# Layer 0's cross-attention: one ring of eight PSUM banks, and maxima and exponentials of two heads at a time

## The chip, the cores and the metric

The kernel runs on one core of a Trainium2 chip. Five engines share the work: TensorE (PE; PEld is its loading of weights), VectorE (DVE), ScalarE (ACT), GpSimd (POOL) and SyncE (SP). The metric is device time in microseconds. The kernel before took 2884.81 us, the median of three runs (2878.84 to 2887.44).

## The reference

A decoder of two layers on 32 sequences of 100 tokens of width 256, all in float32. Each layer is self-attention, cross-attention to a context of 361 rows of width 128, and a feed-forward part with experts, each on a layer norm and with a residual. The change lies in the cross-attention of layer 0, with 16 heads of 16:

```
Q = (x @ Wq.T).reshape(B, xN, NUM_HEADS, HEAD_DIM)
KV = (z @ Wkv.T).reshape(B, zN, 2, NUM_HEADS, HEAD_DIM)
K = KV[:, :, 0]
V = KV[:, :, 1]
attn = jnp.einsum('bqhd,bkhd->bhqk', Q, K) * SCALE
attn = jax.nn.softmax(attn, axis=-1)
O = jnp.einsum('bhqk,bkhd->bqhd', attn, V).reshape(B, xN, DIM)
return O @ Wo.T
```

## The kernel before, in words

The method `l0_xattn` does this part. T is 100 tokens, L is 361 context rows, which are also held as NKC = 3 chunks of KC0 = 121, and P is 128 partitions. Weights (`wB`), context (`cT`, three buffers, loaded two sequences ahead on SP's queue), keys `ks`, values `vs` and the negated maxima `ms` (three buffers each) lie in SBUF.

The 16 heads of a sequence are worked on in four groups: `c` chooses eight heads, and `j` the even or the odd ones of them. The four heads of one `j` lie in four groups of 32 partitions, so that four matmuls with 32 rows can run beside each other. A loop over `M` = 2b + c has 64 full turns for 32 sequences `b`, and two more that finish. The softmax takes the scores twice: once as tokens by context rows, to get each token's maximum, and once turned, as context rows by tokens, with the maximum already subtracted through the query. One turn of the loop issues on PE, in this order:

- `maxima(M - 1)` (L585): two transposes of the negated maxima, which DVE adds to the query (L587, tile `q2`).
- `scores(M, 0)`: four matmuls into four PSUM banks (128 partitions by 512 float32 each), `k,qT` in the profile. DVE reduces each bank to its negated maximum (L577).
- `turned(M - 1, 0)`: twelve matmuls into four banks, `q,k` in the profile; they need `q2`. ACT takes the exponential of each bank (L599, tile `e`), POOL adds two and then the third chunk (L603, L604, tile `es`).
- `values(M - 2)`: the products with the values (L613) and the sums of exponentials (L620) into one bank, which ACT copies (L625, tile `zs`). DVE takes a reciprocal (L630) and POOL multiplies (L634) in a later turn.
- `scores(M, 1)` and `turned(M - 1, 1)`: the same for the other half, j = 1.
- Extras: `keys` of the next sequence (`cT,wB` in the profile; ACT copies them, L549) always first; for c = 0 the output projection of an earlier tile (`wB,zT`; DVE adds it, L283) and two chunks of `vals` (`wB,cT`; ACT copies them, L562); for c = 1 `queries` in half of the sequences (L542) and the third chunk of `vals`. In some turns a tile's norm is turned (L253) or its gates are computed (L1517 and on).

The order on PE is that of the program, written out by hand (`manual_schedule`); the order on DVE, ACT and POOL is set by a scheduler, which keeps the dependencies. The eight PSUM banks are one pool with the tag `t`: `bank()` hands out the next of eight buffers, whatever it is for, and a buffer's next user waits until all users of the one before are done with it. L178 is the line of the helper `mm`, which issues most matmuls, so the operands' names tell them apart.

Of the kernel before, what the change touches and what calls it, by code (L numbers as in the profile page):

```python
# [9 lines left out]
F32 = mybir.dt.float32  # L10
I32 = mybir.dt.int32
U32 = mybir.dt.uint32
AF = mybir.ActivationFunctionType
ALU = mybir.AluOpType
AX = mybir.AxisListType

P = 128
NB = 32
T = 100
# [5 lines left out]
L = 361  # L25
NKC = 3
KC0, KC = 121, 124
# [94 lines left out]
class Kernel:  # L122
    def __init__(self, ctx, tc, a):
        self.ctx, self.tc, self.nc, self.a = ctx, tc, tc.nc, a
        nc = tc.nc
        self.n_evac = self.stored = 0
        self.const = ctx.enter_context(tc.tile_pool(name="const", bufs=1))
        self.wts = ctx.enter_context(tc.tile_pool(name="wts", bufs=1))
        self.lnp = ctx.enter_context(tc.tile_pool(name="ln", bufs=2))
        self.norms, self.norm_of, self.norm_after = {}, {}, None  # L130
        self.x = self.const.tile([P, NF, D], F32, tag="x", name="x_sb")
        xd = a["x"].rearrange("b t d -> (b t) d").rearrange("(f p) d -> p f d", p=P)

        def load_x(f, n=4):
            n = min(n, NF - f)
            nc.sync.dma_start(self.x[:, f : f + n, :], xd[:, f : f + n, :])

        self.load_x = load_x
        load_x(0, 2)
        load_x(2, 2)  # L140
        self.xnT = self.const.tile([P, NK, NT], F32, tag="xnT", name="xnT")
        self.ident = self.const.tile([P, P], F32, tag="ident", name="ident")
        make_identity(nc, self.ident)


    def banks(self, name, **n):

        self.n_banks = n
        return self.tc.tile_pool(name=f"ps{name}", bufs=1, space=bass.MemoryType.PSUM)

    def bank(self, tag):
        if tag not in self.n_banks:
            tag = "t"
        return self.psum.tile([P, 512], F32, tag=tag, name=f"ps_{tag}", bufs=self.n_banks[tag])
# [315 lines left out]
    def l0_xattn(self):  # L470
        nc, tc, a = self.nc, self.tc, self.a
        with ExitStack() as st:
            self.psum = st.enter_context(self.banks("l0x", t=8))
            w = self.wts.tile([P, 3584], F32, tag="wB", name="wB0")
            wq = w[:, :512].rearrange("p (k n) -> p k n", k=NK)
            wk, wv = w[:, 512:768], w[:, 768:1024]
# [40 lines left out]
            ks = [cp.tile([P, 2, 2, LP0], F32, tag=f"k{i}", name=f"k{i}") for i in range(3)]  # L517
            ms = [cp.tile([T, 2, P], F32, tag=f"m{i}", name=f"m{i}") for i in range(3)]
# [9 lines left out]
            ctx, q, q2, e, es = {}, {}, {}, {}, {}  # L528
            self.z_begin(pool, 2)

            def load(b):
                ctx[b] = pool.tile([CD, LP], F32, tag="cT", name="cT", bufs=3)
                nc.sync.dma_start(ctx[b], a["ctxT"][:, b, :])

            def queries(b0, c):
                if c == 0:
                    q[b0 // 4] = pool.tile([P, 2, 2, 4 * T], F32, tag="qT", name="qT")
                pm = self.bank_t()[:, : 4 * T]
                self.mm(pm, [(wq[:, k, c * P : (c + 1) * P], self.xn_of(k, b0, 4)) for k in range(NK)])
                t = q[b0 // 4]  # L540
                for j in range(2):
                    nc.scalar.activation(t[:, c, j, :], pm, AF.Copy, scale=quarter[:, j : j + 1])  # L542

            def keys(b, c):
                pm = self.bank_t()[:, :L]
                self.mm(pm, [(wk[:, c * P : (c + 1) * P], ctx[b][:, :L])])
                t = ks[b % 3]
                for j in range(2):
                    nc.scalar.activation(  # L549
                        t[:, c, j, :L], pm, AF.Identity, bias=one[:, j : j + 1], scale=own[:, j : j + 1]  # L550
                    )

            def vals(b, c0, n):
                pm = self.bank_t()[:KC0, : n * D].rearrange("p (c d) -> p c d", c=n)
                for i in range(n):
                    c = c0 + i
                    self.mm(pm[:, i, :], [(ctx[b][:, c * KC0 : (c + 1) * KC0], wv)])
                pv = pm.rearrange("p c (h j d) -> p c h j d", j=2, d=16)
                v = vs[b % 3][:, c0 : c0 + n].rearrange("p c (h j) e -> p c h j e", j=2)
                for j in range(2):  # L560
                    for i in range(n):
                        nc.scalar.copy(v[:, i, :, j, 16 * j : 16 * j + 16], pv[:, i, :, j, :])  # L562

            def rows_of(r):
                return slice(32 * r, 32 * r + 32)


            def scores(M, j):
                b, c = divmod(M, 2)
                cols = slice((b % 4) * T, (b % 4 + 1) * T)  # L570
                ps = [self.bank("r")[:T, :L] for _ in range(4)]
                for r in range(4):
                    self.mm(ps[r], [(q[b // 4][rows_of(r), c, j, cols], ks[b % 3][rows_of(r), c, j, :L])])
                m = ms[M % 3]
                for r in range(4):
                    o = 32 * r + 16 * (1 - j)
                    got = nc.vector.tensor_reduce(m[:, j, o : o + 1], ps[r], AX.X, ALU.max, negate=True)  # L577
                return got

            def maxima(M):  # L580
# [7 lines left out]

            def turned(M, j):
                b, c = divmod(M, 2)  # L590
                ps = [self.bank("r")[:KC0, : NKC * T] for _ in range(4)]
                for i in range(NKC):
                    for r in range(4):
                        self.mm(ps[r][:, i * T : (i + 1) * T], [(
                            ks[b % 3][rows_of(r), c, j, i * KC0 : (i + 1) * KC0], q2[M][rows_of(r), j, :]
                        )])
                t = e[M, j] = pool.tile([KC0, 4, NKC, T], F32, tag="e", name="e", bufs=5)
                for r in range(4):
                    nc.scalar.activation(t[:, r], ps[r].rearrange("p (c t) -> p c t", c=NKC), AF.Exp)  # L599

                n = L - 2 * KC0
                s = es[M, j] = pool.tile([KC0, 4, T], F32, tag="es", name="es", bufs=4)
                nc.gpsimd.tensor_tensor(s, t[:, :, 0, :], t[:, :, 1, :], ALU.add)  # L603
                nc.gpsimd.tensor_tensor(s[:n], s[:n], t[:n, :, 2, :], ALU.add)  # L604
# [31 lines left out]
            def out(f):  # L636
                self.out_proj(f, wo)
                self.norm_stats(f, EDGES)
# [37 lines left out]
            with tc.manual_schedule(engines={mybir.EngineType.PE}):  # L676
                load(0)
                load(1)
                for c in range(2):
                    queries(0, c)  # L680
                for c in range(2):
                    keys(0, c)
                vals(0, 0, 2)
                vals(0, 2, 1)
                last = 2 * NB
                for M in range(last + 2):
                    b, c = divmod(M, 2)
                    if c == 0:
                        if b + 2 < NB:
                            load(b + 2)  # L690
                        ex = extras(b)
                    if 0 < M <= last:
                        maxima(M - 1)
                    if M in norms:
                        f, *at = norms[M]
                        f(*at)
                    for j in range(2):

                        got = scores(M, j) if M < last else None
                        if j == 0 and M > 2:  # L700
                            divided(M - 3, zs, got)
                        if 0 < M <= last:
                            turned(M - 1, j)
                        if j == 0 and M > 1:
                            zs = values(M - 2)
                    if M == last + 1:
                        divided(M - 2, zs, None)
                    for i in (0, 2, 1):
                        if ex[3 * c + i]:
                            ex[3 * c + i]()  # L710
                    if M not in norms or len(later) > 3:
                        for _ in range(1 + (len(later) > 3)):
                            if later:
                                later.popleft()()
                out(NF - 1)
                while later:
                    later.popleft()()


    def l1_xattn_weights(self):  # L720
# [1484 lines left out]
```

## Time and profile before

| | |
|---|---|
| median of three runs | 2884.81 us (2878.84 to 2887.44) |
| the profiled execution | 2912.63 us, its span 2910.9 us |
| busy over the span | PE 96%, DVE 60%, ACT 48%, POOL 32% |
| granted clock, mean | 0.982 |
| the loop of this part | about 536 to 1011 us of the span |
| maxima, L577 | 512 instructions, 525 ns each, 239.6 us busy |
| exponentials, L599 | 512 instructions, 425 ns each, 173.8 us busy |
| copies of values, L562 | 192 instructions, 300 ns each, 40.0 us busy |

Times of single instructions are durations from start to end. Instructions that follow each other on DVE or ACT overlap, so that the distance of two starts is shorter than the duration. "Waits" name an engine that sat idle, the instruction that ended its idle time, the total in us, the number of times and the longest. Matmul ends are modelled, and so PE counts as busy a little longer than it is.

### The profile page before, as it was taken

The numbers are of one execution on the slowest core, as the hardware profiler recorded it, in microseconds if no ns is written. First come the engines' busy times: TensorE is split into PE (matmuls) and PEld (weight loads), VectorE is DVE, ScalarE is ACT, GpSimd is POOL, SyncE is SP. The second block draws the span as 40 slices with busy tenths as digits, with TensorE's granted clock in tenths as the row PEclk, the third lists the DMA queues.
The fourth block names the chain that finished last, engine by engine and source line by source line (L and its number), as shares of the span: only waits on it lengthen the run. The fifth ranks groups of instructions, "written<-read, shape, count | busy, mean of one in ns | idle before, by whom it ended". The sixth has DMA issues, their size and how long they took to land. (4 is left out here: it accounts for less than half of the span.)

```text
span 2910.9 us, 66193 instructions
## 1 busy us (share of the span) xinstructions
PE 2793.5 (96%) x25908; PEld 2156.8 (74%) x25908; DVE 1760.9 (60%) x5057; ACT 1393.0 (48%) x4210; POOL 920.7 (32%) x1080
## 2 busy tenths in 40 slices
PE   8999999999999998999999999999999999999893
PEld 7888888777777756888885677777777777776672
DVE  7666666677777732222226877667676666776453
ACT  5465545666666611222223225656565556567120
POOL 3222212466565544222221230021311302223373
PEclk9999999999999999999999999999999999999997
DMA  7444333000000033655552000010000000000496
GB/s 246 128 142 151 131 139 120 21 16 16 16 15 14 5 120 117 205 196 199 209 206 86 24 2 10 9 45 19 23 15 9 15 9 14 10 12 6 116 215 188
DMA packets 130035, 235.44 MB, mean 81 GB/s; under 512 B 40074, under 2 KB 105285, under 8 KB 122928
## 3 DMA queue, kind: packets, MB, share of 16 engines
q1 hardware_dynamic: 99648, 136.98, 15.1%
q0 software_dynamic: 26784, 90.83, 9.7%
q8 instruction: 209, 3.42, 0.5%
q10 hardware_dynamic: 3280, 3.28, 0.3%
q14 instruction: 114, 0.93, 0.1%
HBM read 152.12 MB, written 111.18 MB: 90 GB/s over the span
## 5 line engine op out<-in xcount | busy, mean ns | idle before, releaser
L1801 POOL DMA_INDIRECT x_d<-xr,slot x200 | 195.0, 975 | 673.0 <-ACT eT L838 597.1
L178 PE MATMUL ps_t<-xnT,wA 128*128 128x200 f32 (+1 forms) x1608 | 322.5, 347 | 1.6 <-DMA wA<-in_wq 0.9
L178 PE MATMUL ps_t<-cT,q 128*128 128x361 f32 (+1 forms) x832 | 307.2, 472 | 0.0
L838 ACT COPY eT<-ps_t 124x384 f32<-124x384 f32 x400 | 191.5, 487 | 225.9 <-PE ps_t L837 220.7
L178 PEld LDWEIGHTS ps_t<-xnT,wA 128*128 128x128 f32 x1608 | 272.9, 191 | 29.5 <-issue 12.7
L828 ACT ACTIVATE wBx<-ps_t,m 128x361 f32<-128x361 f32 x400 | 227.8, 570 | 119.4 <-DVE m L825 109.9
L577 DVE TENSOR_REDUCE m<-ps_t 100x1 f32<-100x361 f32 x512 | 239.6, 525 | 48.5 <-PE ps_t L178 48.3
L178 PE MATMUL ps_t<-xT,w 128*128 128x256 f32 (+1 forms) x1276 | 260.2, 363 | 0.7 <-ACT xT L172 0.7
L178 PEld LDWEIGHTS ps_t<-xT,w 128*128 128x128 f32 x1276 | 223.6, 190 | 36.2 <-issue 9.3
L825 DVE TENSOR_REDUCE m<-ps_t 128x1 f32<-128x361 f32 x400 | 210.8, 528 | 59.9 <-PE ps_t L178 55.5
L837 PEld LDWEIGHTS ps_t<-ident,wBx 128*124 128x124 f32 x1200 | 150.3, 139 | 117.7 <-issue 71.0
L599 ACT ACTIVATE e<-ps_t 121x300 f32<-121x300 f32 x512 | 173.8, 425 | 120.7 <-PE ps_t L178 120.6
L384 ACT ACTIVATE e<-s,m 100x100 f32<-100x100 f32 x512 | 185.6, 364 | 66.2 <-DVE m L378 66.1
L388 POOL TENSOR_TENSOR e<-e,rz 100x400 f32<-100x400 f32 x128 | 109.1, 853 | 329.9 <-PE ps_t L178 218.7
L837 PE MATMUL ps_t<-ident,wBx 128*124 128x128 f32 x1200 | 196.7, 275 | 3.6 <-DVE top L1741 2.3
L178 PE MATMUL ps_t<-wA,cT 128*124 128x512 f32 x384 | 195.6, 597 | 0.0
L1448 DVE TENSOR_TENSOR h<-ps_t,g 128x256 f32<-128x256 f32 (+1 forms) x145 | 58.3, 402 | 188.4 <-ACT g L1447 180.0
L830 DVE TENSOR_SCALAR wBx<-wBx,sums 128x361 f32<-128x361 f32 x400 | 165.3, 413 | 9.4
L178 PEld LDWEIGHTS ps_t<-q,k 32*121 32x121 f32 x3072 | 128.4, 183 | 36.8 <-issue 11.9
L849 PEld LDWEIGHTS ps_t<-eT,v 124*64 124x64 f32 x3072 | 136.7, 138 | 22.0 <-issue 13.9
L849 PE MATMUL ps_t<-eT,v 124*64 124x100 f32 x3072 | 143.7, 251 | 5.5 <-issue 4.8
L1447 ACT ACTIVATE g<-ps_t 128x256 f32<-128x256 f32 (+1 forms) x145 | 53.0, 366 | 190.8 <-PE ps_t L178 164.1
(333 smaller groups left out, 5625.4 us busy)
## 6 DMA issues: line engine op xcount, KB each, us to landing
x_d<-fill SPq DMA_DIRECT2D x16, 1284.0 KB
we<-in_wexp SPq DMA_DIRECT2D x32, 384.0 KB
cT<-in_ctxT SPq DMA_DIRECT2D x64, 186.0 KB
xe_d<-zero SPq DMA_DIRECT2D x8, 1028.0 KB
xe<-x_d SPq DMA_DIRECT2D x24, 321.0 KB
sum<-fill SPq DMA_DIRECT2D x10, 640.0 KB
yk<-y_d SPq DMA_DIRECT2D x25, 256.0 KB
xe<-xe_d SPq DMA_DIRECT2D x24, 257.0 KB
```

What stands on the lines that cost most here:

```text
L178: self.nc.tensor.matmul(out, lhsT=l, rhs=r, start=(i == 0), stop=(i == n - 1))
L384: nc.scalar.activation(t[:, i, :], s[:, i, :], AF.Exp, bias=m[:, i : i + 1], accum_out=rz[:, i : i + 1])
L388: nc.gpsimd.tensor_tensor(t[:, h, :], t[:, h, :], self.last(rz[:, h], T), ALU.mult)
L577: got = nc.vector.tensor_reduce(m[:, j, o : o + 1], ps[r], AX.X, ALU.max, negate=True)
L599: nc.scalar.activation(t[:, r], ps[r].rearrange("p (c t) -> p c t", c=NKC), AF.Exp)
L825: self.after = nc.vector.tensor_reduce(m, ps, AX.X, ALU.max, negate=True)
L828: nc.scalar.activation(t, ps, AF.Exp, bias=m, accum_out=z)
L830: nc.vector.tensor_scalar(t, t, z, None, ALU.mult)
L837: nc.tensor.transpose(pt[:, c, :], es[n % 5][:, c * KC : (c + 1) * KC], self.ident)
L838: self.after = nc.scalar.copy(eT[:, :, o : o + P], pt)
L849: nc.tensor.matmul(pz[64 * j : 64 * j + 64, i, :], lhsT=v[:, c, h * 64 : (h + 1) * 64], rhs=eT[:, c, o : o + T], start=(c == 0), stop=(c = ...
L1801: got = nc.gpsimd.indirect_dma_start(out=self.x1_d[:, :], out_offset=bass.IndirectOffsetOnAxis(ap=slot[:, j, k : k + 1], axis=0), in_=xr[: ...
```

## The change

All eight banks become one tile, `ring`. `take(n)` hands out the next bank, or the next two from an even bank on, skipping one if need be; `bank()` takes a single one of the ring while this part runs. Scores and turned scores are written to pairs of banks, in the same order of matmuls. One DVE instruction reduces the two banks of a pair to the maxima of two heads, and one ACT instruction takes the exponentials of two heads. The copies of two chunks of values become one for each half `j`. Behind the part, `ring` is dropped.

```diff
@@ __init__
+        self.ring = None
@@
+    def take(self, n):
+
+        self.ring_at += -self.ring_at % n
+        i = self.ring_at % 8
+        self.ring_at += n
+        return self.ring[:, i : i + n, :]
+
     def bank(self, tag):
+        if self.ring is not None:
+            return self.take(1)[:, 0, :]
         if tag not in self.n_banks:
             tag = "t"
@@ l0_xattn
-            self.psum = st.enter_context(self.banks("l0x", t=8))
+            self.psum = st.enter_context(self.banks("l0x", t=1))
+            self.ring, self.ring_at = self.psum.tile([P, 8, 512], F32, tag="t", name="ps_t"), 0
@@ vals
                 for j in range(2):
-                    for i in range(n):
-                        nc.scalar.copy(v[:, i, :, j, 16 * j : 16 * j + 16], pv[:, i, :, j, :])
+                    nc.scalar.copy(v[:, :, :, j, 16 * j : 16 * j + 16], pv[:, :, :, j, :])
@@ scores
-                ps = [self.bank("r")[:T, :L] for _ in range(4)]
+                ps = [self.take(2)[:T, :, :L] for _ in range(2)]
                 for r in range(4):
-                    self.mm(ps[r], [(q[b // 4][rows_of(r), c, j, cols], ks[b % 3][rows_of(r), c, j, :L])])
-                m = ms[M % 3]
-                for r in range(4):
-                    o = 32 * r + 16 * (1 - j)
-                    got = nc.vector.tensor_reduce(m[:, j, o : o + 1], ps[r], AX.X, ALU.max, negate=True)
+                    self.mm(
+                        ps[r // 2][:, r % 2, :], [(q[b // 4][rows_of(r), c, j, cols], ks[b % 3][rows_of(r), c, j, :L])]
+                    )
+                m = ms[M % 3][:, j, :].rearrange("p (r i) -> p r i", r=4)[:, :, 16 * (1 - j)]
+                for i in range(2):
+                    got = nc.vector.tensor_reduce(m[:, 2 * i : 2 * i + 2], ps[i], AX.X, ALU.max, negate=True)
                 return got
@@ turned
-                ps = [self.bank("r")[:KC0, : NKC * T] for _ in range(4)]
+                ps = [self.take(2)[:KC0, :, : NKC * T] for _ in range(2)]
                 for i in range(NKC):
                     for r in range(4):
-                        self.mm(ps[r][:, i * T : (i + 1) * T], [(
+                        self.mm(ps[r // 2][:, r % 2, i * T : (i + 1) * T], [(
                             ks[b % 3][rows_of(r), c, j, i * KC0 : (i + 1) * KC0], q2[M][rows_of(r), j, :]
                         )])
                 t = e[M, j] = pool.tile([KC0, 4, NKC, T], F32, tag="e", name="e", bufs=5)
-                for r in range(4):
-                    nc.scalar.activation(t[:, r], ps[r].rearrange("p (c t) -> p c t", c=NKC), AF.Exp)
+                for i in range(2):
+                    nc.scalar.activation(
+                        t[:, 2 * i : 2 * i + 2].rearrange("p r c t -> p r (c t)"), ps[i], AF.Exp
+                    )
@@ the end of l0_xattn
+            self.ring = None
```

## The prediction

> **What bounds the kernel now.** I read the engines' rows over the whole span, then the engines' busy time in the stage that the change touches, then what its instructions wait for, and last the order of time inside one step. A step is one turn of the loop over `M`: step 1 begins at 535.9 us with its two L585 transposes, step 64 at 1010.8.
>
> ```profile
> PE   8999999999999998999999999999999999999893
> ```
> ```profile
> 536.00:1011.00 475.00, 464.50 (x8722) 361.29 (x8720) 358.69 (x871) 322.48 (x928) 285.56 (x360) 0.99 0.05 14
> ```
>
> The columns of the second are the stretch, its length, then busy us of PE, PEld, DVE, ACT and POOL, the granted clock (0.99), the DMA share and GB/s. PE has work in 464.5 of 475.0 us. DVE (76%) and ACT (68%) are not full and DMA plays no part. So time goes into this stage only where PE is held up, and out of it only where a holdup is removed. The wait view of the same stretch for weight loads, the first thing that a held PE doesn't start, names who holds it (us in total, times, longest):
>
> ```profile
> PEld ps_t L178 <- DVE m L577: 9.6, 54, 0.5
> PEld ps_t L178 <- ACT v L562: 8.1, 14, 1.1
> PEld ps_t L613 <- DVE m L577: 8.0, 14, 1.4
> ```
>
> 54 times a projection or score waits, about 0.18 us each, for a maximum (L577) to give a bank back; 14 times the values (L613) do. One step shows where (start, length):
>
> ```profile
> 682.22 0.34 PE L585 MATMUL ps_t<-ident,m 100*128 100x100 f32 x2
> 682.48 0.87 PE L178 MATMUL ps_t<-k,qT 32*100 32x361 f32 x8
> 683.17 0.94 PE L178 MATMUL ps_t<-q,k 32*121 32x100 f32 x24
> 684.05 1.24 PE L613 MATMUL ps_t<-e,v 121*32 121x100 f32 x48
> 685.10 0.53 PE L620 MATMUL ps_t<-es,ones 121*32 121x100 f32 x16
> 685.56 0.87 PE L178 MATMUL ps_t<-k,qT 32*100 32x361 f32 x8
> 686.25 0.79 PE L178 MATMUL ps_t<-q,k 32*121 32x100 f32 x24
> 687.03 0.87 PE L178 MATMUL ps_t<-cT,wB 128*128 128x361 f32 x2
> ```
> ```profile
> 683.37 1.85 DVE L577 TENSOR_REDUCE m<-ps_t 100x1 f32<-100x361 f32 x4 [0.41 <-PE ps_t L178]
> 685.33 0.78 DVE L630 RECIPROCAL zs<-zs 128x100 f32<-128x100 f32 x1
> 686.44 1.86 DVE L577 TENSOR_REDUCE m<-ps_t 100x1 f32<-100x361 f32 x4 [0.34 <-PE ps_t L178]
> ```
>
> PE runs scores (`k,qT`), turned scores (`q,k`), values and sums, then scores and turned scores of the other half, then the next keys (`cT,wB`). With eight banks in turn, the values take the bank of the first half's first score, and the keys that of the second half's first score: in the listing of the built program 61 of the 64 groups of values and 60 of the 62 of keys in the loop wait for just that maximum. In time: the first maximum of the second half starts at 686.44 and lasts 0.525 (group row below), so it ends at 686.965, and the keys start at 687.03, 0.065 later. They sit exactly on that maximum. The values don't: the same sum for the first half gives 683.37 + 0.525 + 0.065 = 683.96, and they start at 684.05, after turned scores that waited 0.09 for ACT's copies.
>
> **The change, part by part.**
>
> *Maxima by pairs.* 512 instructions of 100x361 become 256 of 100x(2x361). No such row exists; these are the nearest:
>
> ```profile
> L577 DVE TENSOR_REDUCE m<-ps_t 100x1 f32<-100x361 f32 x512 | 239.6, 525 | 48.5 <-PE ps_t L178 48.3
> L378 DVE TENSOR_REDUCE m<-s 100x8 f32<-100x800 f32 x64 | 63.1, 985 | 1.9
> ```
>
> (985 - 525) / (800 - 361) = 1.048 ns for an element, so 722 elements take 525 + 361 x 1.048 = 903 ns. Bounds: below, 722 elements with nothing fixed, 0.757; above, two single ones, 1.05. I take 0.903, as L378 also reduces several rows at once. Single ones start 0.44 apart, pairs would start 0.44 + 0.38 = 0.82 apart: 256 x (0.88 - 0.82), some 16 us of DVE's time, is saved. None of it is PE's: DVE is idle 24%, and what PE waits for is the *first* bank, which now comes back with its neighbour at 0.903 instead of alone at 0.525: 0.378 later. The new banks keep these neighbours: in the changed program 62 groups of values and all 62 of keys wait for the first pair's maximum of their half. What is queued behind on PE is, for the values, the sums and the whole second half of the step; for the keys, the output projection, the next values' projection and the next step's transposes. All are late by as much, and ACT's copies of keys and values and DVE's L587 follow them.
>
> *Keys:* +0.378 in each step. Over the trace's steps 2 to 62 by the rule "start = first maximum's start + 0.903 + 0.065, or the old start if that is later": 56 of the 61 steps pay 0.12 to 0.40 (nearly all 0.38); five (19, 24, 35, 51 and 57) pay nothing, since late exponentials or other work hold the turned scores longer. The sum is **20.7 us**.
>
> *Values:* the same rule, but the place has a cover: turned scores need 0.78 us unhindered (shortest found), and mostly take more, waiting for ACT's queue (exponentials, copies of keys, queries, values). That is 28 us of stall in these steps, and while PE stands there for ACT the maximum goes on. Where that queue doesn't depend on the keys' start, it also swallows the 0.38 by which the keys of the step before were late. By kind of step:
> - odd, turned scores 0.87 (15 steps, like the one shown): 683.37 + 0.903 + 0.065 = 684.34 against 684.05, +0.29 in 12, nothing in the three with late exponentials: +3.5.
> - odd, 0.78 (7 steps): +0.38 in 6: +2.3.
> - odd, about 1.45 (7) and step 57: ACT was the limit; the old stall shrinks by the keys' lateness until the maximum is the limit: -0.29 in six, +0.39 in one: -1.3.
> - even (31 steps, 1.07 to 2.7): the previous keys' 0.38 comes off, the maximum puts it back: -0.38 to +0.39, together +0.2. In step 10, say, values began 2.13 us into the step; now, with the step begun 0.38 later, they begin 2.12 into it.
> Sum **+4.6 us**. Without the cover it would be 0.38 in each of 62.
>
> *Exponentials by pairs*, 512 to 256. ACT's rows:
>
> ```profile
> L599 ACT ACTIVATE e<-ps_t 121x300 f32<-121x300 f32 x512 | 173.8, 425 | 120.7 <-PE ps_t L178 120.6
> L409 ACT COPY zT<-ps_t 128x400 f32<-128x400 f32 x16 | 7.8, 491 | 30.6 <-PE ps_t L178 30.6
> ```
>
> A copy of 176 elements takes 309 ns, so (491 - 309) / 224 = 0.81 ns an element, and a pair 425 + 300 x 0.81 = 0.67 us. Four singles end 1.36 after the first starts (0.30 apart); two pairs, 0.55 apart, at 1.22. Bounds for these 0.14 us: none gained (singles already overlap), and 0.3 (one start interval). *Copies of v*, 192 to 128: 128 elements start 0.157 apart, 256 then 0.26: 0.1 us saved in even steps. Both shorten ACT's queue, which ends a stall only in the four even steps where ACT stays last (8, 16, 38, 46): about -0.5. What waits for the first pair (the other half's scores) comes 1.5 us of values and sums later, and a pair ends at 0.67: hidden; without the values it would cost 0.25.
>
> *Ring.* Pairs start on even banks, so one bank is skipped after the values and one before the scores of some steps. A skipped bank makes later users come one earlier; the values, keys and both halves keep the previous users named above, with the slack shown, so 0. Order on PE, POOL and SP is unchanged, no DMA is added or moved; on DVE only a few routing operations of L1521 to L1546 change places with maxima. At the end of the stage the next one's first matmuls are already queued behind the last projections: 0.
>
> Sum: 20.7 + 4.6 - 0.5 = **+25 us**. After the stage PE is again full (100% from 1200 to 1500), so the delay is passed on whole.
>
> The row behind the main term is DVE's 76% in this stage, with PE waiting on it 68 times. The Trainium skill (Perfetto Trace Analysis, Optimizing Scalar/DVE Operations) says that grouping into larger operations pays if the engine is saturated, and that where Scalar or Vector are not saturated but cause bubbles on others, breaking instructions up may let work complete sooner. It speaks against this change: by its first clause, with its some 125 ns of overhead per DVE instruction on PSUM, 256 fewer would save 32 us of DVE (an estimate), by its second nothing is gained and PE's bubbles grow; the rows give the size.
>
> **Reference.** The profiled execution took 2912.6 us (span 2910.9), 1.0% over the median 2884.81 of three runs. 25 / 2910.9 = 0.86%, on the median 2884.81 x 1.0086 = **2910 us**.
>
> **Rivals.**
> 1. *No cover*: the stalls on ACT stay and both delays come on top: 62 x 0.378 x 2 = 47 us, 2931. For: PE runs in order. Against: stall and maximum run at the same time. 0.10.
> 2. *Not slower, ACT's relief wins*: stalls of turned scores (28 us) shorten by 0.14 to 0.24 in the 37 steps where ACT sets them, -7 us, 2878, if a pair's maximum returns its banks about as soon as a single one. It decides below 0.66 us for a pair, where the rule's sum for keys and values is 6 to 7 us. For: stalls on `ACT v` are 8.1 us of weight-load waits. Against: 722 elements at L378's rate. 0.12.
> 3. *Hidden anyway*: the delay is made up at the stage's end or later, where PE waits for routing and for DMA (12.4 us for `xe` near the end); 0 to +8, about 2888. Against: those waits follow from PE's own results. 0.06.
> 4. *The change doesn't do what it says*: the one tile makes each write wait for all readers of all eight banks, some 5 us a step, +300. Against: the built program's waits name single banks. 0.02.
>
> **Chances and range.** The forecast has 0.70. 0.3% (8.7 us) is about what a measurement of this kernel can tell from no change. Slower: 0.68 of the forecast (0.02 of it at its low end is within) + rivals 1 and 4 = 0.80. Same: 0.02 + 0.05 of rival 2 + rival 3 = 0.13. Faster: 0.07, the rest of rival 2. With a pair at its lower bound 0.757 the rule gives +12.6 us (2897), at 1.05 +41.5 (2926). I take 2893 to 2926: 4 us lower for what ACT's relief may add at the low end.
>
> **What would show it.** L588 of the changed kernel with 256 instructions of about 0.90 us. Keys starting some 1.16 us after the second half's turned scores begin instead of 0.78, in nearly every step; values about 0.97 after their half's first maximum starts; weight loads' waits for maxima some 40 us in total instead of 18; the stage about 25 us longer, the rest the same. Turned scores' waits for ACT should shrink. Wrong if a pair takes under 0.66 us, if keys and values start as early as before, or if the added time lies outside the stage.

## The result, and the profile after

| | before | after |
|---|---|---|
| median, four runs each on one chip | 2885.38 us (2878.84 to 2887.44) | 2914.31 us (2912.75 to 2915.09) |
| ratio, 95% interval | | 1.0103 [1.0089, 1.0118] |
| span of the profiled execution | 2910.9 us | 2912.3 us |
| the loop: first to last transpose of the maxima (L585, L596) | 474.9 us | 503.7 us |
| maxima | 512 of 525 ns, 239.6 us busy | 256 of 905 ns, 221.9 us busy |
| exponentials | 512 of 425 ns, 173.8 us busy | 256 of 668 ns, 157.7 us busy |

The kernel became 28.9 us slower, and the loop alone 28.8 us longer. The two spans hardly differ because the profiled execution of before was 1.0% above its median. So the loops are compared below, and medians only between kernels that ran side by side. One run of the experiment with ring and pairs of maxima alone took 9333 us at a granted clock of 0.296 and is left out of its median.

The row of PE on the page of after, then the loop's busy times (length, busy us of PE, PEld, DVE, ACT and POOL, clock, DMA share, GB/s):

```profile
PE   8999999999989889999999999999999999999992
```
```profile
537.00:1040.50 503.50, 452.25 (x8721) 346.37 (x8720) 342.78 (x618) 310.24 (x614) 285.27 (x360) 1.00 0.05 13
```

PE did the same work (8721 matmuls, 8722 before) with some 51 us of idle time instead of 10.5; the loop grew by less than this difference because PE's modelled busy time is 12 us lower. DVE has 16 us and ACT 12 us less to do in the loop and POOL's work is the same: engines with less work, and a longer stage. The merged instructions in the view of groups (instructions | busy, mean ns | idle before, by whom):

```profile
L588 DVE TENSOR_REDUCE m<-ps_t 100x2 f32<-100x722 f32 x256 | 221.9, 905 | 66.1 <-PE ps_t L188 65.2
L610 ACT ACTIVATE e<-ps_t 121x600 f32<-121x600 f32 x256 | 157.7, 668 | 128.3 <-PE ps_t L188 116.2
```

The waits of weight loads in the loop of after (us in total, times, longest):

```profile
PEld ps_t L626 <- DVE m L588: 34.7, 54, 1.5
PEld ps_t L188 <- DVE m L588: 33.0, 60, 0.9
```

The maxima now hold weight loads for 67.7 us instead of 17.6, about equally at the values (L626, 54 times instead of 14) and at the keys (56 of the 60 waits of L188, instead of 44). Step 21, the one shown before, on PE and on DVE:

```profile
692.17 0.34 PE L596 MATMUL ps_t<-ident,m 100*128 100x100 f32 x2
692.44 0.87 PE L188 MATMUL ps_t<-k,qT 32*100 32x361 f32 x8
693.13 0.82 PE L188 MATMUL ps_t<-q,k 32*121 32x100 f32 x24
694.37 1.24 PE L626 MATMUL ps_t<-e,v 121*32 121x100 f32 x48 [0.42 <-DVE m L588]
695.43 0.53 PE L633 MATMUL ps_t<-es,ones 121*32 121x100 f32 x16
695.88 0.87 PE L188 MATMUL ps_t<-k,qT 32*100 32x361 f32 x8
696.57 0.79 PE L188 MATMUL ps_t<-q,k 32*121 32x100 f32 x24
697.75 0.88 PE L188 MATMUL ps_t<-cT,wB 128*128 128x361 f32 x2 [0.39 <-DVE m L588]
```
```profile
693.41 1.73 DVE L588 TENSOR_REDUCE m<-ps_t 100x2 f32<-100x722 f32 x2 [0.49 <-PE ps_t L188]
695.24 0.78 DVE L643 RECIPROCAL zs<-zs 128x100 f32<-128x100 f32 x1
696.78 1.73 DVE L588 TENSOR_REDUCE m<-ps_t 100x2 f32<-100x722 f32 x2 [0.77 <-PE ps_t L188]
```

The first pair of the second half starts at 696.78; 0.905 and the 0.065 of before later is 697.75, when the keys start. For the values, 693.41 + 0.905 + 0.065 = 694.38, and they start at 694.37. In nearly every step the keys now come 1.18 us after the turned scores begin instead of 0.785. One number is not as expected: the first half's first pair starts 1.235 into the step, where the first single maximum started 1.15 into it.

The added time by place, over steps 2 to 62 (the rest of the loop gives 0.8 us back), from the starts on PE in the two traces:

| | predicted | after |
|---|---|---|
| second halves, up to the keys | +20.7 | +18.1 |
| first halves, odd, turned scores 0.87 before (15 steps) | +3.5 | +5.6 |
| first halves, odd, 0.78 before (7 steps) | +2.3 | +7.8 |
| first halves, odd, about 1.45, and step 57 (8 steps) | -1.3 | -0.4 |
| first halves, even (31 steps) | +0.2 | +0.3 |
| values and sums themselves | 0 | -1.8 |
| ACT's relief | -0.5 | in the rows above |
| sum | +25 | +29.6 |

The -1.8 is not the change's. Before, values and sums take 1.51 us in every one of these steps but 24 (1.99) and 58 (2.82), and in the profile of before the granted clock was 0.69 from 705 to 710 us and 0.66 from 965 to 970, where these two lie. In a second profile of the same kernel (the first experiment below), at a granted clock of 1.00 in both places, they take 1.51 us there too, as they do after.

The row of the seven steps stands out. In them DVE also works on routing. The DVE timeline of after around step 23, which begins at 707.29:

```profile
707.48 0.17 DVE L1531 COPY lg<-ps_t 128x16 f32<-128x16 f32 x1 [1.80 <-PE ps_t L188]
707.70 0.37 DVE L598 TENSOR_TENSOR q<-ps_t,qT 128x200 f32<-128x200 f32 x1
707.98 0.23 DVE L1535 MAX8 top<-lg 128x8 f32<-128x8 f32 x2
...
708.58 0.17 DVE L1537 CAST tf<-ti 128x4 f32<-128x4 uint32 x1
708.79 0.26 DVE L1539 TENSOR_TENSOR hot<-io,tf 128x16 f32<-128x16 f32 x2
709.08 0.17 DVE L1542 TENSOR_TENSOR sel<-hot,hot 128x16 f32<-128x16 f32 x1
709.17 0.91 DVE L588 TENSOR_REDUCE m<-ps_t 100x2 f32<-100x722 f32 x1
```

DVE's order is fixed when the kernel is built, and with pairs the scheduler put L1537, L1539 and L1542 ahead of the step's first pair. The pair starts 709.17 - 707.29 = 1.88 into the step, though its scores are done some 0.65 earlier. Before, the same instructions lay between the four single maxima, and the first of these started 1.18 into the step.

### The profile page after: what moved, and what is told of

Same layout as the page of the kernel before. It is cut to its first block, busy times and chain, and to the rows that moved or that the text cites. A ratio compares the mean times of both kernels' runs of the same rounds, so it can differ in the third digit from the quotient of the medians.

```text
span 2912.3 us, 65888 instructions
## 1 busy us (share of the span) xinstructions
PE 2766.2 (95%) x25908; PEld 2133.6 (73%) x25908; DVE 1745.9 (60%) x4801; ACT 1378.9 (47%) x3890; POOL 920.4 (32%) x1080
## 5 line engine op out<-in xcount | busy, mean ns | idle before, releaser
L188 PE MATMUL ps_t<-xnT,wA 128*128 128x200 f32 (+1 forms) x1608 | 321.6, 347 | 1.6 <-DVE x_sb L293 0.6
L188 PE MATMUL ps_t<-cT,q 128*128 128x361 f32 (+1 forms) x832 | 307.3, 472 | 0.0
L188 PEld LDWEIGHTS ps_t<-xnT,wA 128*128 128x128 f32 x1608 | 271.8, 191 | 29.9 <-issue 12.7
L588 DVE TENSOR_REDUCE m<-ps_t 100x2 f32<-100x722 f32 x256 | 221.9, 905 | 66.1 <-PE ps_t L188 65.2
L188 PE MATMUL ps_t<-xT,w 128*128 128x256 f32 (+1 forms) x1276 | 260.2, 364 | 0.7 <-ACT xT L182 0.7
L188 PEld LDWEIGHTS ps_t<-xT,w 128*128 128x128 f32 x1276 | 223.8, 190 | 36.0 <-issue 9.3
L610 ACT ACTIVATE e<-ps_t 121x600 f32<-121x600 f32 x256 | 157.7, 668 | 128.3 <-PE ps_t L188 116.2
L188 PE MATMUL ps_t<-wA,cT 128*124 128x512 f32 x384 | 195.5, 597 | 0.0
L188 PEld LDWEIGHTS ps_t<-q,k 32*121 32x121 f32 x3072 | 115.7, 180 | 36.5 <-ACT v L572 11.0
L843 DVE RECIPROCAL sums<-sums 128x1 f32<-128x1 f32 x400 | 63.8, 160 | 126.4 <-ACT wBx L842 125.0
```

The source lines that it names most:

```text
L188: self.nc.tensor.matmul(out, lhsT=l, rhs=r, start=(i == 0), stop=(i == n - 1))
L588: got = nc.vector.tensor_reduce(m[:, 2 * i : 2 * i + 2], ps[i], AX.X, ALU.max, negate=True)
L610: nc.scalar.activation(t[:, 2 * i : 2 * i + 2].rearrange("p r c t -> p r (c t)"), ps[i], AF.Exp)
```

## The experiments

Each ran beside the kernel before on one chip. Three chips were used, with medians of the kernel before of 2906.7, 2909.77 and 2908.0 us. "The loop" is the one of the table above, read from one profile of each kernel.

### Before, once more

> The kernel before once more, for a second profile. Its first profiled execution was 27 us longer than its median, and behind the loop it took 1900 us where the changed kernel takes 1872. If that was this one execution: a span near 2884, the loop (first to last L585) 475 us again, and about 1872 behind it. If the change itself shortened what comes behind the loop: about 1900 again.

Measured: span 2904.6, loop 473.0, 1895 behind it. The span expected did not come, since on this chip the kernel before has a median of 2906.7. The loop's 475 is confirmed within 2 us, and what lies behind it changes with chip and execution: ratios are taken on one chip only.

### Single maxima, all else as in the change

```diff
-                for i in range(2):
-                    got = nc.vector.tensor_reduce(m[:, 2 * i : 2 * i + 2], ps[i], AX.X, ALU.max, negate=True)
+                for r in range(4):
+                    got = nc.vector.tensor_reduce(m[:, r : r + 1], ps[r // 2][:, r % 2, :], AX.X, ALU.max, negate=True)
```

> The changed kernel with maxima of one head at a time again (ring, pairs of exponentials and merged copies stay). If the pair's maximum, which returns its first bank 0.38 us later, costs the time: ratio 0.996 to 1.000, keys again 0.78 us after the second half's turned scores begin, weight loads' waits for maxima 18 us or less instead of 67. If the skipped banks of the ring or the pairs of exponentials cost it: 1.008 or more stays.

Measured: 0.9979 [0.9969, 0.9989], 2901.37 us against 2906.7; loop 469.5. The waits of weight loads in its loop:

```profile
PEld ps_t L188 <- DVE m L588: 9.7, 56, 0.5
PEld ps_t L626 <- DVE m L588: 7.6, 11, 1.4
```

They are as small as before the change. The maxima by pairs are the whole loss, and without them the rest of the change is a small gain.

### Ring and pairs of maxima alone

The exponentials and the copies of `v` are single again:

```diff
-                for i in range(2):
+                for r in range(4):
                     nc.scalar.activation(
-                        t[:, 2 * i : 2 * i + 2].rearrange("p r c t -> p r (c t)"), ps[i], AF.Exp
+                        t[:, r].rearrange("p c t -> p (c t)"), ps[r // 2][:, r % 2, :], AF.Exp
                     )
```

> Ring and pairs of maxima, but exponentials and copies of values one at a time as before. If the pair's maximum costs the time: ratio 1.009 to 1.013. If the exponentials or the copies do: within 1.002. If each has a part: between.

Measured: 1.0101 [1.0081, 1.0121], 2935.88 (median of three runs) against 2906.7; loop 504.2. The pairs of maxima suffice for the loss. Merging exponentials and copies, worth 0.2% above, is worth nothing here. That fits: where a maximum sets the start on PE, a shorter queue on ACT ends no wait.

### Pairs over half the columns

```diff
-                    got = nc.vector.tensor_reduce(m[:, 2 * i : 2 * i + 2], ps[i], AX.X, ALU.max, negate=True)
+                    got = nc.vector.tensor_reduce(m[:, 2 * i : 2 * i + 2], ps[i][:, :, :181], AX.X, ALU.max, negate=True)
```

> The changed kernel, with each pair's maximum over the first 181 of 361 columns (the other columns are left out of the maxima). The instruction still covers two banks, waits alike and returns both at once, but lasts about 0.53 us instead of 0.90. If the duration up to the first bank's return is what costs: ratio 0.996 to 1.002. If it is the pairing itself (two banks returned together, the second wait that comes before a pair's maximum): 1.006 or more.

Measured: 0.9981 [0.9971, 0.9990]; loop 471.3. The group of its maxima in the loop:

```profile
L588 DVE TENSOR_REDUCE m<-ps_t 100x2 f32<-100x362 f32 x252 | 124.4, 530 | 95.0 <-PE ps_t L188 92.8 <-ACT k L560 1.5 <-ACT xnT L182 0.4
```

The pairing is unchanged, and the instructions are as long as single ones: the loss is gone. So neither two banks in one instruction nor the ring costs the time, but the duration until the first bank comes back. What pairing costs without that shows in the seven routing steps: their first halves up to the values sum to 17.6 us, against 12.6 with single maxima, since the order on DVE is that of the change.

### Two heads single, two as a pair

```diff
-                for i in range(2):
-                    got = nc.vector.tensor_reduce(m[:, 2 * i : 2 * i + 2], ps[i], AX.X, ALU.max, negate=True)
+                for r in range(2):
+                    nc.vector.tensor_reduce(m[:, r : r + 1], ps[0][:, r, :], AX.X, ALU.max, negate=True)
+                got = nc.vector.tensor_reduce(m[:, 2:4], ps[1], AX.X, ALU.max, negate=True)
```

> The changed kernel, but of the four heads of a half the first two are reduced one at a time and only the last two as a pair (384 instructions). If only the time until the first bank comes back matters: ratio 0.997 to 0.999, as with all maxima single (0.998), and DVE's maxima busy some 8 us less than there. If two banks that come back together cost something anywhere else: 1.002 or more.

Measured: 1.0000 [0.9991, 1.0009], 2910.71 against 2909.77; loop 472.7. This lies between the two expectations: the loss goes, but so does the gain of 0.2%. The waits of weight loads (from 540 to 1005 us) tell single maxima (L588) and the pair (L589) apart:

```profile
PEld ps_t L188 <- DVE m L588: 8.9, 56, 0.2
PEld ps_t L188 <- DVE m L589: 7.7, 16, 0.8
PEld ps_t L627 <- DVE m L588: 7.3, 8, 1.4
```

The middle row is new. 14 of its 16 waits, 7.0 of the 7.7 us, are of the second half's scores (`k,qT`), which take the third and fourth bank of the first half's scores and so wait for the pair. In the seven steps with routing on DVE they start 2.11 to 2.19 us after the values instead of 1.51. Besides, in 16 steps the loop loses 0.12 to 0.22 us behind the turned scores, 2.6 us in all; there a third piece of work, such as a norm's transpose, takes the third bank of the second half. The third bank has slack in most steps, not in all.

### A long first maximum without pairs or ring

The kernel before, with the first maximum of each half going over its bank twice, so that it reads 722 elements:

```diff
-                    got = nc.vector.tensor_reduce(m[:, j, o : o + 1], ps[r], AX.X, ALU.max, negate=True)
+                    src = ps[r]
+                    if r == 0:
+                        src = self.mid(ps[r], 2)
+                    got = nc.vector.tensor_reduce(m[:, j, o : o + 1], src, AX.XY if r == 0 else AX.X, ALU.max, negate=True)
```

> The kernel before (eight separate banks, everything single), with the first of the four maxima of each half taken twice over its own bank, 722 elements instead of 361, so that it lasts about 0.90 us. No pair, no ring. If the lateness of the first bank is the whole cause: ratio 1.008 to 1.013, keys 1.16 us after the second half's turned scores begin. If the pairing or the ring is needed for the loss: within 1.002.

Measured: 1.0086 [1.0072, 1.0101], 2935.8 against 2909.77; loop 501.7. The long maxima, and the waits of weight loads, both from 540 to 1005 us:

```profile
L580 DVE TENSOR_REDUCE m<-ps_t 100x1 f32<-100x722 f32 x117 | 106.1, 907 | 28.5 <-PE ps_t L178 28.3
```
```profile
PEld ps_t L178 <- DVE m L580: 29.3, 62, 0.9
PEld ps_t L616 <- DVE m L580: 21.5, 46, 1.8
```

A late first bank by itself brings most of the loss in the kernel before. By the places of the table (second halves; first halves of the four kinds; values and sums): +20.2; +4.3, +2.7, -1.3, +0.3; -0.8, together +25.4. The prediction's rule gave 20.7; 3.5, 2.3, -1.3, 0.2; 0, together 25.3. This is the rule by itself, and it holds row by row, within 0.8 us. The -0.8 has the same source as the -1.8 above: steps at a lowered clock, one here (24) and two before (24 and 58).

### The ring alone

Exponentials, maxima and copies all single, on the ring.

> The changed kernel with maxima, exponentials and copies of values all single again: only the ring and its skipped banks stay. If skipping costs nothing: ratio 0.999 to 1.001, and the 0.2% that the kernel with single maxima gained belongs to the exponentials and copies. If skipping costs what they give: 1.002 or more.

Measured: 1.0004 [0.9995, 1.0013]; loop 474.7. The ring and its skipped banks cost nothing. With the kernel of single maxima (469.5) this gives the gain of merged exponentials and copies: 5.2 us, read from one profile each, where two profiles of the kernel before differ by 1.9.

### Values ahead of the turned scores

The kernel of single maxima, with another order on PE:

```diff
-                        if 0 < M <= last:
-                            turned(M - 1, j)
                         if j == 0 and M > 1:
                             zs = values(M - 2)
+                        if 0 < M <= last:
+                            turned(M - 1, j)
```

> The kernel with single maxima on the ring, and in each step the values ahead of the first half's turned scores. The 1.5 us of values and sums then cover the wait of turned scores for ACT's queue and for the query with the maxima (some 23 us over the loop), but the second half's turned scores come 1.5 us earlier behind the first half's exponentials, whose second pair would be about 0.6 us late for them in many steps. If the first weighs more: 0.992 to 0.997; if the second does: 1.000 to 1.006.

Measured: 1.0111 [1.0096, 1.0125], 2943.79 against 2909.77; loop 503.8. This missed both expectations. The waits of weight loads from 540 to 1005 us:

```profile
PEld ps_t L188 <- ACT e L610: 58.7, 116, 1.7
```

The order frees the values of the maxima, but the second half's scores and turned scores then follow the first half's turned scores directly, without the 1.5 us of values and sums between. All 116 of these waits are of turned scores (`q,k`), whose banks ACT's exponentials still read: the second turned scores start 0.935 us after the second scores instead of 0.688, and the keys follow 1.37 us later instead of 0.785 (medians).

### Pairs in the second half alone, and in the first half alone

```diff
-                for i in range(2):
-                    got = nc.vector.tensor_reduce(m[:, 2 * i : 2 * i + 2], ps[i], AX.X, ALU.max, negate=True)
+                if j == 1:
+                    for i in range(2):
+                        got = nc.vector.tensor_reduce(m[:, 2 * i : 2 * i + 2], ps[i], AX.X, ALU.max, negate=True)
+                else:
+                    for r in range(4):
+                        got = nc.vector.tensor_reduce(m[:, r : r + 1], ps[r // 2][:, r % 2, :], AX.X, ALU.max, negate=True)
```

and the same with `j == 0`.

> The changed kernel with its maxima single in the first half (j = 0) and by pairs in the second half alone, so that only the bank that the keys take comes back late. The kernel with all maxima single had a loop of 469.5 us and 0.998 of the time before, with all by pairs 503.7 and 1.010. Theory (the keys' lateness falls into stalls of the next step's turned scores, unless the first half's pair puts it back): by the prediction's rule for starts with 0.903 in the second half and 0.525 in the first, keys +20.7 and values -8.9 us, so a loop some 12 us over 469.5, about 481 (478 to 485), and a ratio of 1.001 to 1.003. Rival A (the prediction's two terms each stand alone): +20.7, a loop of 490, ratio 1.005. Rival B (the two halves cost the same): +17, a loop of 487, ratio 1.004.

> The changed kernel with its maxima by pairs in the first half (j = 0) and single in the second, so that only the bank that the values take comes back late. Theory: by the rule for starts with 0.903 in the first half and 0.525 in the second, values +9.6 and keys +0.1 us; if the 0.085 us by which a first half's pair starts later than a single maximum counts in some 60 steps, up to 5 us more: a loop of 479 to 485 us against 469.5, ratio 1.001 to 1.004. Rival A (the prediction's terms each stand alone): +4.6, a loop of 474, ratio 0.9995. Rival B (the halves cost the same): +17, a loop of 487, ratio 1.004.

Measured: 1.0035 [1.0022, 1.0049] and 1.0036 [1.0023, 1.0048]; loops 487.0 and 486.0, so 17.5 and 16.5 us over the kernel of single maxima: rival B's numbers. Together the two come to 34.0 us, what pairs in both halves cost on this ring (503.7 - 469.5 = 34.2). Waits of weight loads from 540 to 1005 us, with pairs in the second half (pairs L589, single L592; values L630):

```profile
PEld ps_t L188 <- DVE m L589: 31.0, 54, 0.9
...
PEld ps_t L630 <- DVE m L592: 5.8, 7, 1.2
```

and with pairs in the first half:

```profile
PEld ps_t L630 <- DVE m L589: 31.8, 47, 1.5
...
PEld ps_t L188 <- DVE m L592: 8.6, 54, 0.2
```

Each pair holds its own follower, and the other one waits no longer than with single maxima. That the two cost the same is no law, as the places (steps 2 to 62, against the kernel of single maxima) show. Pairs in the second half: second halves +23.6, first halves -5.4, values and sums -1.3 (step 24 of the kernel of single maxima, at a granted clock of 0.75). The cover is real, but smaller than the 8.9 expected. The merged exponentials and copies had taken 3.6 us of the first halves' time already (133.9 us with the ring alone, 130.3 with single maxima), which would account for it. Pairs in the first half: first halves +20.3, of which +7.6 in the seven routing steps; second halves -3.5. With pairs in the second half alone the routing steps' first halves stay at 12.6 us. The DVE timeline of that kernel, whose step 23 begins at 701.80, shows the first maximum between the routing instructions:

```profile
702.89 0.16 DVE L1540 FIND_INDEX8 ti<-top,lg 128x8 uint32<-128x8 f32 x1
702.98 0.53 DVE L592 TENSOR_REDUCE m<-ps_t 100x1 f32<-100x361 f32 x1
703.43 0.16 DVE L1541 CAST tf<-ti 128x4 f32<-128x4 uint32 x1
703.50 0.53 DVE L592 TENSOR_REDUCE m<-ps_t 100x1 f32<-100x361 f32 x1
```

## Why the prediction was right, and where it was not

- **The cause** was as predicted: the pair gives its first bank back 905 - 525 = 380 ns later (predicted 378), the values and the keys wait for it, PE does nothing else meanwhile. Taking the pairs away (0.9979), leaving them alone (1.0101), shortening them (0.9981) and lengthening a single maximum (1.0086) all say so.
- **The keys** were right: 0.39 later in nearly every step (predicted 0.378). Their sum is 18.1 instead of 20.7; in steps 19, 35 and 51, where late exponentials hold the second half, it became 0.62 shorter instead of staying equal. Step 24 became 0.68 shorter, but not by the change: the prediction put its slowness down to late exponentials or other work, and it was the granted clock of 0.69 in the profile of before (in the second profile, at 1.00, its second half took 1.47 us instead of 2.54; there that of step 58 took 2.80 instead of 1.78, so the growth of the second halves against it is 18.1 us again).
- **The values** were mis-sized: 4.6 predicted, 13.3 measured. The rule was right, as the long first maximum shows, but its input, the start of the first maximum, was taken over from before, and it moved. First, "a few routing operations of L1521 to L1546 change places with maxima" was costed at nothing, as a change of order on an engine with 24% idle time. In seven steps it makes the first pair some 0.65 us late. Those steps cost 7.8 instead of 2.3; the run with short pairs gives 5.0 us for the order alone. Second, pairs of the first half start 85 ns later after their scores. The values of the first odd kind are later by 0.37 in all 15 steps, where 0.29 in 12 was predicted.
- **The waits** of weight loads for maxima were 68 us, not some 40. They grew by 50 us and the loop by 29: at the values of the even steps such a wait now stands 24 times instead of 7, though on the whole they start hardly later (+0.3). The prediction's sign that turned scores' waits for ACT should shrink did not come. In the wait view weight loads wait for ACT's `v`, `k`, `qT` and `e` 24.6 us in the loop of after, against 14.6 before; a part of this may be naming, as waits without a releaser ("issue") fell from 21.0 to 15.2.
- **ACT's relief** of 0.5 us was small within the change, as predicted (with and without it, loops of 503.7 and 504.2, too close for profiles that differ by 1.9 in themselves). Without pairs it is 5.2 us.
- **The ring** at 0 was right (1.0004).
- **The rivals.** *No cover*: the long first maximum has the cover the rule gave, -1.3 in the third odd kind and +0.3 in the even steps. *ACT's relief wins*: a pair takes 0.905, not under 0.66; but the relief is the 0.2% by which single maxima on the ring beat the kernel before. *Hidden anyway*: the loops differ by 28.8 and the medians by 28.9, and behind the loop the kernel before and the one with ring and pairs of maxima alone take 1895 and 1893 us on one chip. *Whole-tile waits*: the ring alone costs nothing.

The total of 25 us fell 4 us short of the measured growth because two costs of some 9 us together were left out, against 4.4 us by which the second halves, values and sums came out lower. 1.8 of these 4.4 us, at values and sums, are the lowered clock in the profile of before; against its second profile the rows sum to +31.4 us. So the mechanism was right, but that the sum came this close is in part luck: the left-out costs and the shorter second halves pull opposite ways.

The Trainium skill (Perfetto Trace Analysis, Optimizing Scalar/DVE Operations) says that where Vector is not saturated but causes bubbles on other engines, breaking up instructions may let work complete sooner. The runs agree: on the same ring, 256 more maxima make the loop 34 us shorter. The prediction's estimate that 256 fewer would save 32 us of DVE came out at about half: their busy time fell by 17.7 us (239.6 to 221.9).

The best version of these runs is the ring with merged exponentials and copies and single maxima: 0.9979 [0.9969, 0.9989] of the time before.

## What to carry to other kernels

Before merging instructions of an engine that isn't full, ask what it gives back and who is waiting for the first piece: a merged instruction returns everything at its end. Read which buffer the next user on the bottleneck takes; merge only where that buffer has slack (here the exponentials, not the maxima). And compare the built order on that engine line by line: a merged instruction can no longer be started between others, so the scheduler may put small work ahead of it that used to lie between its parts.

## What the runs showed that was not expected

- The 85 ns by which a first half's pair starts late have two parts. With single exponentials (ring and pairs of maxima alone), 246 of the 256 pairs wait for PE alone in the trace, and most start 1.19 us into the step, 42 ns after a single maximum's 1.15. A pair needs the second head's score too, which may be why. With merged exponentials, 177 of 256 carry a wait on ACT as well, and most start 1.236 us into the step, another 44 ns later. There DVE's sequencer runs a separate semaphore instruction ahead of the pairs, 179 of them with 21 ns each, against 9 with single exponentials. In step 21 it waits for PE and ends 1.192 us into the step, just where a pair starts with single exponentials; this pair starts at 1.235. ACT's last exponentials before it had ended 2.8 us earlier, so their wait was already satisfied. These times suggest that the separate wait costs the 44 ns; no run tried it by itself.
- For DVE's maximum only the number of elements counted: 722 took 905 ns as two rows and 907 as one bank read twice; 362 as two rows took 530, and 361 as one 525.
